# Two adjacency layers on one core: the order of the first batch's opening, and GpSimd for three kinds of small work

## The chip, the cores and the metric

The kernel runs on one core of a Trainium2 chip. A core has TensorE (PE: matrix products, written to the accumulation memory PSUM), VectorE (DVE), ScalarE (ACT), GpSimd (POOL) and SyncE (SP, which here only issues DMAs). Each engine runs its own instructions strictly in order; between engines, order is kept by semaphores. The metric is the device time of one launch in microseconds (us), as the median of several runs.

## The reference

A batch of 16 graphs of 1024 nodes with 128 features passes two layers, both in float32; a layernorm over the features follows the residual addition of each. `adj` holds zeros and ones.

```python
# layer 0, per batch
h = x @ Ww.T + Wb
e = (h @ A) @ h.T;  e = e + e.T
scores = where(adj > 0, e, 0)
attention = softmax(scores, axis=1) * adj        # along the first node index
hp = relu(attention @ h)
ic, fc, oc = (sigmoid(hp @ w_u + x @ w_x) for each gate)
x = layernorm(x + oc * tanh(ic * hp + fc * x))

# layer 1, per batch, 4 heads
h = x @ conv_w + conv_b
Ah = tanh(adj * (h @ attn_w @ h.T))
x = layernorm(x + relu(relu(mean over heads of relu(Ah @ h)) + x))
```

## The kernel before

All work goes in tiles of 128 rows, so a batch has eight row tiles j = 0 to 7 of 128 x 1024 scores. The host passes x also as its transpose `xT`, and adj as `adjT`.

**The weights' chain.** Scores need only the symmetric matrix A + A^T. The kernel makes a_sym = A + A^T, s_ww = a_sym times Ww, and q_w = Ww^T s_ww, so that the scores are products of a query projection `qT` = q_w applied to xT (with a bias column `c_col`) and xT itself; the bias part left over is a column that h carries along. For that the rows of h have G = 132 columns: 128 for h, three for the gates' `x @ w_x`, one for the bias part of the score. The matrix that makes them is `wwT_g`: Ww^T, then `gate_x` (three columns, made by a product of `rows_x` with an identity and a copy), then `c_col`. What is added to each row is `wb_row`: the bias Wb, zeros, and in the last column a number that is made out of `sb_col` = a_sym Wb by one more product (`finish_weights`, L163). Each of these small products is one TensorE instruction pair into a tile of PSUM (the helper `small`, four rotating buffers of 512 columns) and a copy out by VectorE or ScalarE; the chain is lines 142 to 166. Two of them, for `c_col` (L154) and for `sb_col` (L156), write columns of one tile, `p_c`. `gates_x` (L159) is called later, after the first query projection.

**Layer 0 of batch 0** is at the front of the kernel with nothing beside it but the first pieces of batch 1. `layer0` (L283) returns a dictionary of pieces, each a function that issues a few instructions, and the order in which the strings name them is the order in which the instructions stand in every engine's queue. The pieces that matter here, with their lines:

- `Q0`, `Q1` (L306): the two halves of the query projection on TensorE, copied out with the bias: for batch 0 by ScalarE (Q0) and VectorE (Q1).
- `H0` to `H2` (L323) and `h0` to `h2` (L333): products of xT with `wwT_g` for three, three and two row tiles, and VectorE's addition of `wb_row` (L335). The last addition also copies the 24 gate columns out of h (L341).
- `E j` (L391): the edge tile adj > 0. For batch 0 it is made by VectorE in bfloat16, for the others by GpSimd.
- `S j` (L343): the scores of row tile j from the diagonal to the right; ScalarE drains them from PSUM into the big tile `R`, and adds h's last column as bias (L353), so the first drain waits for `h0`. For batch 0, S0 is one piece and S1 is split into S1.0 and S1.1.
- `T j` (L359, L380): the scores left of the diagonal are transposes of earlier ones; for batch 0 by TensorE through PSUM with a copy back by ScalarE (L368, L369, L385, L386).
- `A j` (L401): VectorE masks the row tile and takes its maximum in one instruction (L405), negates the maximum (L410), and ScalarE takes the exponential in place and its sum z (L412). The mask overwrites what `T j` reads, so it waits for that.
- `B j` (L414): VectorE takes 1/z (L420); h over that sum, called `hz`, is made by VectorE for j = 0, 1, 6, 7 of batch 0 (L422) and otherwise by ScalarE (L424); VectorE multiplies the exponentials by adj (L427); and TensorE accumulates row tile j - 1 (`back`, L431, L435), with hz as the weights.
- `R`, `P`, `G`: the last accumulation and relu (L440), the rows of h' (L446), the gates (L499). Inner, outer and norm pieces (I, O, V, N) follow, then batch 0's x for layer 1.

The order of the opening is lines 725 to 767, written by hand, a string per stretch. The loads stand first: xT in two halves, the eight adjacency tiles of batch 0, x, batch 1's xT, the late weights, and batch 1's adjacency tiles, all on SP's queue. ScalarE's queue issues A, Wb as a column and the three `rows_x` (L73 to L80); GpSimd's issues Wb into `wb_row` (L91).

**From there on** the 16 batches go through layer 1 in 32 steps each (`layer1_step`, L613: scores on TensorE, times adj on VectorE, tanh on ScalarE, accumulation on TensorE). Between the steps, two tables by step number (`BETWEEN`, `AHEAD`, L771 and L776) put in the layer 0 pieces of the next two batches. The additions `h0 h1 h2` of a later batch stand at step 14 of `AHEAD`, next to `Y` (a GpSimd product, L467) at step 14 and `F` (GpSimd again, L493) at step 16.

Of the kernel before, what the change touches and what calls it, by code (L numbers as in the profile page):

```python
# [24 lines left out]
def two_layer_adjacency_kernel(  # L25
# [19 lines left out]
    nc = tc.nc  # L45
    B, N, D = x.shape
    H = conv_w.shape[0]
    assert D == P and N % 512 == 0
    NB = N // P
# [11 lines left out]
    def small(name):  # L61
        return ps_sc.tile([P, 512], F32, tag="sc", name=name)
# [4 lines left out]
    ident = consts.tile([P, P], F32, name="ident")  # L67
# [8 lines left out]
    wb_col = consts.tile([P, 1], F32, name="wb_col")  # L76
    nc.scalar.dma_start(wb_col, Wb.rearrange("(d o) -> d o", o=1))
    rows_x = sb.tile([3, P], F32, tag="s1", name="rows_x", bufs=4)
# [14 lines left out]
    gate_u, gate_x = ident_g[:, D : D + 3], wwT_g[:, D : D + 3]  # L93
# [33 lines left out]
    a_sym = sb.tile([P, P], F32, tag="hz", name="a_sym", bufs=4)  # L127
# [3 lines left out]
    sb_col = consts.tile([P, 1], F32, name="sb_col")  # L131
# [10 lines left out]
    pa, pw, ps, pc = small("p_a"), small("p_ww"), small("p_s"), small("p_c")  # L142
# [8 lines left out]
    pq, px = small("p_q"), small("p_x")  # L151
# [1 line left out]
    nc.vector.tensor_copy(q_w, pq[:, :P])  # L153
    nc.tensor.matmul(pc[:, 0:1], s_ww, wb_col, start=True, stop=True)  # L154
    nc.vector.tensor_copy(c_col, pc[:, 0:1])
    nc.tensor.matmul(pc[:, 1:2], a_sym, wb_col, start=True, stop=True)  # L156
    nc.vector.tensor_copy(sb_col, pc[:, 1:2])

    def gates_x():  # L159
        nc.tensor.matmul(px[:, :3], rows_x, ident[:3, :3], start=True, stop=True)  # L160
        nc.vector.tensor_copy(gate_x, px[:, :3])

    def finish_weights():  # L163
        pt = small("p_bsb")
        nc.tensor.matmul(pt[:, :1], b_wide, sb_col, start=True, stop=True)
        nc.vector.tensor_copy(wb_row[:, G - 1 : G], pt[:, :1])

    def join_weights():

        nc.vector.tensor_sub(cw, cw_in, cw_last)  # L170
        pt = small("p_cwT")
        for hd in range(H):
            nc.tensor.transpose(pt[:, ts(hd, P)], cw[:, hd, :], ident)
        nc.scalar.copy(cwT.rearrange("p h f -> p (h f)"), pt)
        yield
        pt = small("p_caT")
        for hd in range(H):
            nc.tensor.matmul(pt[:, ts(hd, P)], aw[:, hd, :], cwT[:, hd, :], start=True, stop=True)
        nc.scalar.copy(caT.rearrange("p h f -> p (h f)"), pt)
        yield  # L180
        pt = small("p_m")
        for hd in range(H):
            nc.tensor.matmul(pt[:, ts(hd, P)], caT[:, hd, :], cwT[:, hd, :], start=True, stop=True)
        nc.scalar.copy(ms.rearrange("p h f -> p (h f)"), pt)
# [98 lines left out]
    def layer0(b):  # L283
# [5 lines left out]
        t = {}  # L289
# [43 lines left out]
        def add_h(g):  # L333
            h, ks = t["h"], GROUPS[g]
            nc.vector.tensor_add(  # L335
                h[:, ks[0] : ks[-1] + 1, :], t["ph", g],
                wb_row.unsqueeze(1).to_broadcast([P, len(ks), G]),
            )
            if g == len(GROUPS) - 1:
                t["gate"] = sb.tile([P, NB, 3], F32, tag="gate", name=f"gate_{b}")  # L340
                nc.vector.tensor_copy(t["gate"], h[:, :, D : D + 3])  # L341

        def score(j, halves=None):  # L343
            if j == 0:
# [69 lines left out]
        def weigh(j):  # L414

            s = t["R"][:, :, j, :]
            adj = adj_t[b, j].rearrange("p (k d) -> p k d", d=P)
            rz = sb.tile([P, 1], F32, tag="rz", name=f"rz_{b}_{j}", bufs=4)
            t["hz", j] = sb.tile([P, D], F32, tag="hz", name=f"hz_{b}_{j}", bufs=4)
            nc.vector.reciprocal(rz, t["z", j])  # L420
            if b == 0 and j in (0, 1, NB - 2, NB - 1):
                nc.vector.tensor_scalar_mul(t["hz", j], t["h"][:, j, :D], rz)  # L422
            else:
                nc.scalar.mul(t["hz", j], t["h"][:, j, :D], rz)  # L424

            for ks in (ts(0, BH), ts(1, BH)) if (b, j) == (0, NB - 1) else [slice(NB)]:
                nc.vector.tensor_mul(s[:, ks], s[:, ks], adj[:, ks])  # L427
            if j:
                back(j - 1)

        def back(j):  # L431
            if j == 0:
                t["acc"] = ps_acc.tile([P, N], F32, tag="acc0", name=f"acc0_{b}")
            for q in range(NH):
                nc.tensor.matmul(  # L435
                    t["acc"][:, ts(q, 512)], t["hz", j], t["R"][:, ts(q, BH), j, :],
                    start=(j == 0), stop=(j == NB - 1),
                )
# [117 lines left out]
        for g in range(len(GROUPS)):  # L556
            pieces[f"H{g}"] = partial(multiply_h, g)
            pieces[f"h{g}"] = partial(add_h, g)
# [7 lines left out]
        for j in range(NB):  # L566
            for name, piece in (
                ("L", load_adj), ("E", find_edges), ("S", score), ("A", mask), ("B", weigh)
            ):
                pieces[f"{name}{j}"] = partial(piece, j)  # L570
            if j + 1 < NB:
                pieces[f"T{j}"] = partial(turn_score, j)
# [4 lines left out]
    def run(pieces, names):  # L577
        for name in names.split():
            if name in pieces:
                pieces.pop(name)()  # L580
# [144 lines left out]
    first, second, join = layer0(0), layer0(1), join_weights()  # L725
# [2 lines left out]
    load_late_weights()  # L728
    run(second, "L0 L1 L2 L3 L4 L5 L6 L7")
    run(first, "Q0")  # L730
    gates_x()
    finish_weights()
    run(first, "E0 H0 h0 E1 E2 S0 T0.0 S1.0 T0.1 S1.1 A0 E3 T1 S2 A1 Q1 E4 H1 h1 B0 T2 S3 A2 E5 B1")
    run(first, "H2 h2 T3 S4 A3 E6 B2")
    run(first, "T4 S5 A4 E7 B3 T5 S6 A5 B4 T6 S7 A6")
    run(second, "Q0")
    run(first, "B5 A7")
    run(second, "H0")
# [136 lines left out]
```

## Time and profile before

| what | value |
|---|---|
| median of 4 runs | 2414.4 us |
| the four runs | 2412.87, 2412.93, 2415.86, 2415.90 us |
| time of the profiled execution | 2412.87 us |
| its span, first to last instruction | 2410.9 us |
| granted TensorE clock, mean | 1.000 |
| TensorE busy | 2398.8 us |
| VectorE busy | 1555.0 us |
| ScalarE busy | 1063.2 us |
| GpSimd busy | 603.3 us |
| GpSimd busy between 5.2 and 47.6 us | 0 |

The profile is one execution as the hardware profiler took it. Busy times are sums of instruction lengths on an engine; in a row of instructions in order of time, the first number is the start in us from the span's start, the second the length; brackets give the idle time of the engine before it, and behind the arrow what ended it. The chain of waits is found by going back from the last instruction: at each step to what released it, or to the instruction before it on its engine. "issue" in it is time in which the engine waited for nothing that the profile shows. Matmul ends are modelled.

### The profile page before, as it was taken

What the parts mean: (1) busy time and instruction counts of PE and PEld (TensorE: products, weight loads), DVE (VectorE), ACT (ScalarE), POOL (GpSimd) and SP (SyncE); (2) the same over time, 40 slices, a digit from 0 to 9 for tenths busy, and PEclk for the clock granted to TensorE, in tenths of its full rate; (3) what the DMA queues carried; (4) which work ended last, traced back from release to release, by engine and by line L of the source; (5) the groups of instructions that cost most, each with busy time, mean ns of one, the idle gap of its engine ahead of it and who ended that gap; (6) DMA issues with size and microseconds to landing.
All of it is one profiled execution on the core that took longest, in us unless ns stands there. A gap on an engine that the chain in (4) does not pass through costs nothing.

```text
span 2410.9 us, 20160 instructions
## 1 busy us (share of the span) xinstructions
PE 2398.8 (100%) x5981; PEld 1095.2 (45%) x5981; DVE 1555.0 (64%) x3280; ACT 1063.2 (44%) x1500; POOL 603.3 (25%) x373
## 2 busy tenths in 40 slices
PE   8999999999999999999999999999999999999999
PEld 5444444444444444444444444444444444444444
DVE  7666666666667666676666665666666576666555
ACT  6544344443444444445344454434444344443333
POOL 1314131241312413123131231312214132141000
PEclk9999999999999999999999999999999999999999
DMA  5334151441514325143242432425234251341010
GB/s 185 79 75 127 36 139 36 95 115 48 127 44 99 102 51 124 49 109 87 60 115 57 113 76 70 105 61 122 62 71 113 53 126 58 79 115 34 18 27 9
DMA packets 474349, 197.04 MB, mean 82 GB/s; under 512 B 414964, under 2 KB 440303, under 8 KB 474240
## 3 DMA queue, kind: packets, MB, share of 16 engines
q1 hardware_dynamic: 455626, 129.03, 22.9%
q0 software_dynamic: 18320, 66.66, 9.4%
q8 instruction: 48, 0.79, 0.1%
q14 instruction: 61, 0.50, 0.1%
q10 hardware_dynamic: 294, 0.07, 0.0%
HBM read 136.19 MB, written 59.51 MB: 81 GB/s over the span
## 4 chain that ended last, share of the span: by engine, by line
PE 98%; DVE 1%; DMA 0%; issue 0%; ACT 0%; POOL 0%; POOLq 0%; DVEq 0%; ACTq 0%
PE sc L630 36%; PE acc L636 36%; PE acc L435 9%; PE sc L350 5%; PE pR L601 5%; PE pT_u L234 5%; PE pR_h L331 1%; PE pT_q L234 1%; DMA adj<-in_adjT_dram 0%; DVE R L405 0%; DVE R L427 0%; DVE st L210 0%; DVE edge L398 0%; DMA a_in<-in_L_gnn_A_dram 0%; DVE u L523 0%
## 5 line engine op out<-in xcount | busy, mean ns | idle before, releaser
L631 DVE TENSOR_TENSOR s<-sc,adj 128x512 f32<-128x512 f32 x1008 | 685.6, 688 | 710.7 <-PE sc L630 689.8
L632 ACT ACTIVATE s<-s 128x1024 f32<-128x1024 f32 x504 | 533.1, 1058 | 1057.4 <-DVE s L631 898.0
L630 PE MATMUL sc<-uT,x1T 128*128 128x512 f32 x2048 | 962.4, 592 | 0.0
L636 PE MATMUL acc<-s,h 128*128 128x512 f32 x2016 | 947.3, 592 | 0.0
L636 PEld LDWEIGHTS acc<-s,h 128*128 128x128 f32 x2016 | 380.5, 190 | 484.7 <-issue 477.5
L630 PEld LDWEIGHTS sc<-uT,x1T 128*128 128x128 f32 x2048 | 386.9, 190 | 469.3 <-issue 403.5
L398 POOL TENSOR_SCALAR edge<-adj 128x1024 uint8<-128x1024 f32 x120 | 332.8, 2774 | 316.1 <-DVE top_None L405 314.0
L214 POOL TENSOR_TENSOR rs<-rs,mhalf 128x8 f32<-128x8 f32 (+3 forms) x35 | 54.0, 1543 | 884.5 <-DVE rs L213 884.5
L435 PE MATMUL acc<-R,hz 128*128 128x512 f32 x512 | 240.8, 593 | 2.3 <-DVE R L427 1.4
L412 ACT ACTIVATE R<-R,nmax 128x1024 f32<-128x1024 f32 x128 | 147.0, 1148 | 84.8 <-DVE nmax L410 75.5
L405 DVE CUSTOM_DVE_ANT_0 R<-R,edge 128x1024 f32<-128x1024 f32 (+1 forms) x128 | 154.8, 1209 | 0.5 <-PE turn L368 0.5
L427 DVE TENSOR_TENSOR R<-R,adj 128x1024 f32<-128x1024 f32 x129 | 154.5, 1198 | 0.0
L435 PEld LDWEIGHTS acc<-R,hz 128*128 128x128 f32 x512 | 96.6, 190 | 124.7 <-issue 115.0
L350 PE MATMUL sc<-xT,qT 128*128 128x512 f32 (+3 forms) x384 | 145.2, 487 | 0.5 <-ACT R L369 0.3
L353 ACT ACTIVATE R<-sc,h 128x512 f32<-128x512 f32 (+1 forms) x192 | 110.7, 580 | 52.0 <-PE sc L350 44.3
L467 POOL TENSOR_TENSOR x1T<-hp,wu_b 128x1024 f32<-128x1024 f32 x45 | 106.3, 2362 | 103.5 <-DVE hws L473 63.7
L234 PE MATMUL pT_u<-x1T,ms 128*128 128x512 f32 x256 | 120.5, 592 | 0.0
L601 PE MATMUL pR<-cw,x1T 128*128 128x512 f32 x256 | 117.6, 598 | 0.0
L350 PEld LDWEIGHTS sc<-xT,qT 128*128 128x128 f32 x384 | 69.6, 190 | 69.6 <-issue 59.8
L300 POOL DMA_DIRECT2D adj<-in_adjT_dram x112 | 65.7, 587 | 92.6 <-DVE s L631 92.6
L654 DVE SCALAR_TENSOR_TENSOR sum<-acc,sum 128x512 f32<-128x512 f32 x95 | 61.3, 687 | 42.1 <-PE acc L636 42.1
L604 ACT COPY h<-pR 128x512 f32<-128x512 f32 x128 | 72.4, 592 | 27.9 <-PE pR L601 26.2
(144 smaller groups left out, 1127.7 us busy)
## 6 DMA issues: line engine op xcount, KB each, us to landing
adj<-in_adjT_dram POOLq DMA_DIRECT2D x112, 512.0 KB, 4.0
adj<-in_adjT_dram SPq DMA_DIRECT2D x16, 512.0 KB, 8.2
x<-in_x_dram SPq DMA_DIRECT2D x16, 512.0 KB, 5.3
xT<-in_xT_dram SPq DMA_DIRECT2D x15, 512.0 KB, 4.8
dram_hp<-turn_hp SPq DMA_DIRECT2D x15, 512.0 KB, 2.6
hp<-dram_hp SPq DMA_DIRECT2D x60, 128.0 KB, 3.3
dram_x<-turn_x SPq DMA_DIRECT2D x15, 512.0 KB, 3.1
x1T<-dram_x SPq DMA_DIRECT2D x60, 128.0 KB, 5.7
```

Of the source, the lines that this page charges most:

```text
L234: nc.tensor.matmul(ps, w, src[:, ts(q, 512)], start=True, stop=True)
L350: nc.tensor.matmul(ps[:, : at - lo], t["qT"][:, ts(j, P)], t["xT"][:, lo:at], start=True, stop=True)
L398: engine.tensor_scalar(m, adj_t[b, j], 0.0, None, ALU.is_gt)
L405: nc.vector.tensor_tensor_reduce(s[:, ks], s[:, ks], t["edge", j][:, ks], 1.0, nmax, ALU.mult, ALU.max, top)
L412: nc.scalar.activation(s, s, AF.Exp, bias=nmax, accum_out=t["z", j])
L427: nc.vector.tensor_mul(s[:, ks], s[:, ks], adj[:, ks])
L435: nc.tensor.matmul(t["acc"][:, ts(q, 512)], t["hz", j], t["R"][:, ts(q, BH), j, :], start=(j == 0), stop=(j == NB - 1),)
L601: nc.tensor.matmul(ps, x1T_t[b][:, ts(k, P)], cw.rearrange("p h d -> p (h d)"), start=True, stop=True)
L630: nc.tensor.matmul(ps, x1T[:, ts(m, P)], uT[:, ts(q, 512)], start=True, stop=True)
L631: nc.vector.tensor_mul(s[:, ts(q, 512)], ps, adj[:, ts(q, 512)])
L632: nc.scalar.activation(s, s, AF.Tanh)
L636: nc.tensor.matmul(acc[:, ts(q, 512)], h1[:, ts(hd, D)], s[:, ts(q, 512)], start=(m == 0), stop=(m == NB - 1),)
```

## The change

- The gate product and its copy (`rows_x` into `gate_x`) move from behind the first query projection into the weights' chain, straight after `c_col`. The product for `sb_col` takes the place behind the projection, now as `weigh_bias`, and writes a column of the gates' tile `p_x` instead of `p_c`.
- `H0` is issued ahead of `finish_weights`, and `h0` ahead of the first edge tile `E0`.
- The edge tiles are spread anew: E1 and E2 stand behind A0 instead of ahead of S0, and every later one moves one place back. `Q1` moves from behind A1 to ahead of T1.
- hz of batch 0 is made by GpSimd for all eight row tiles. The gate columns of every batch are copied by GpSimd.

```diff
     nc.vector.tensor_copy(c_col, pc[:, 0:1])
-    nc.tensor.matmul(pc[:, 1:2], a_sym, wb_col, start=True, stop=True)
-    nc.vector.tensor_copy(sb_col, pc[:, 1:2])
-
-    def gates_x():
-        nc.tensor.matmul(px[:, :3], rows_x, ident[:3, :3], start=True, stop=True)
-        nc.vector.tensor_copy(gate_x, px[:, :3])
+    nc.tensor.matmul(px[:, :3], rows_x, ident[:3, :3], start=True, stop=True)
+    nc.vector.tensor_copy(gate_x, px[:, :3])
+
+    def weigh_bias():
+        nc.tensor.matmul(px[:, 3:4], a_sym, wb_col, start=True, stop=True)
+        nc.vector.tensor_copy(sb_col, px[:, 3:4])
...
                 t["gate"] = sb.tile([P, NB, 3], F32, tag="gate", name=f"gate_{b}")
-                nc.vector.tensor_copy(t["gate"], h[:, :, D : D + 3])
+                nc.gpsimd.tensor_copy(t["gate"], h[:, :, D : D + 3])
...
             nc.vector.reciprocal(rz, t["z", j])
-            if b == 0 and j in (0, 1, NB - 2, NB - 1):
-                nc.vector.tensor_scalar_mul(t["hz", j], t["h"][:, j, :D], rz)
+            if b == 0:
+                nc.gpsimd.tensor_scalar_mul(t["hz", j], t["h"][:, j, :D], rz)
             else:
                 nc.scalar.mul(t["hz", j], t["h"][:, j, :D], rz)
...
     run(first, "Q0")
-    gates_x()
+    weigh_bias()
+    run(first, "H0")
     finish_weights()
-    run(first, "E0 H0 h0 E1 E2 S0 T0.0 S1.0 T0.1 S1.1 A0 E3 T1 S2 A1 Q1 E4 H1 h1 B0 T2 S3 A2 E5 B1")
-    run(first, "H2 h2 T3 S4 A3 E6 B2")
-    run(first, "T4 S5 A4 E7 B3 T5 S6 A5 B4 T6 S7 A6")
+    run(first, "h0 E0 S0 T0.0 S1.0 T0.1 S1.1 A0 E1 E2 Q1 T1 S2 A1 E3 H1 h1 B0 T2 S3 A2 E4 B1")
+    run(first, "H2 h2 T3 S4 A3 E5 B2")
+    run(first, "T4 S5 A4 E6 B3 T5 S6 A5 E7 B4 T6 S7 A6")
     run(second, "Q0")
     run(first, "B5 A7")
```

## The prediction

> **What bounds the kernel now.** I read the page first, its busy table, its slices and its shares of the chain. The span is TensorE's from end to end but for the first slice.
>
> ```profile
> span 2410.9 us, 20160 instructions
> ...
> PE 2398.8 (100%) x5981; PEld 1095.2 (45%) x5981; DVE 1555.0 (64%) x3280; ACT 1063.2 (44%) x1500; POOL 603.3 (25%) x373
> ...
> PE 98%; DVE 1%; DMA 0%; issue 0%; ACT 0%; POOL 0%; POOLq 0%; DVEq 0%; ACTq 0%
> ```
>
> The chain cut to its first 75 us shows where the other 2% lie: pieces with start, length and engine.
>
> ```profile
> 2.94 6.71 DMA adj<-in_adjT_dram
> ...
> 9.67 0.07 DVE edge L398
> ...
> 10.28 0.57 DVE h L335
> ...
> 10.94 0.70 ACT R L353
> ...
> 37.22 0.30 ACT hz L424
> ...
> 37.56 5.55 PE acc L435 x12
> ```
>
> Up to 9.65 the chain waits for the first adjacency tile; then the edge tile and h's first addition stand in line, ScalarE's first score (L353) waits for that addition, VectorE carries 18 to 35 us, and TensorE's last accumulations close batch 0. From 57 on TensorE has no gap, so whatever the first 57 us gain or lose goes to the end unchanged. The changed lines act there, apart from a copy of 24 columns per batch.
>
> Third view: VectorE's instructions in order of time; brackets hold the idle time before and what ended it.
>
> ```profile
> 9.67 0.69 DVE L398 TENSOR_SCALAR edge<-adj 128x1024 bf16<-128x1024 f32 x1 [1.13 <-DMA adj<-in_adjT_dram]
> 10.28 0.56 DVE L335 TENSOR_TENSOR h<-pR_h,wb_row 128x396 f32<-128x396 f32 x1
> ...
> 15.75 1.23 DVE L405 CUSTOM_DVE_ANT_0 R<-R,edge 128x1024 f32<-128x1024 f32 x1 [0.51 <-PE turn L368]
> ...
> 17.79 0.75 DVE L312 TENSOR_SCALAR qT<-pT_q_second,wwT_g 128x512 f32<-128x512 f32 x1 [0.62 <-PE pT_q_second L311]
> ...
> 19.73 0.29 DVE L422 TENSOR_SCALAR hz<-h,rz 128x128 f32<-128x128 f32 x1
> 19.93 1.22 DVE L427 TENSOR_TENSOR R<-R,adj 128x1024 f32<-128x1024 f32 x1
> 21.07 1.22 DVE L405 CUSTOM_DVE_ANT_0 R<-R,edge 128x1024 f32<-128x1024 f32 x1
> ```
>
> The reader sees gaps until 17.79, none that matter from there to 40.9, and that one hz on VectorE sits between a reciprocal and a product. I call mask j "A j", product j "B j" (reciprocal, hz, product), edge tile j "E j".
>
> **Step 1, the weights' chain.** Now the product for c_col, the one for sb_col (both in tile p_c, so the second waits 0.33 for c_col's copy, until 6.37) and the first query projection at 6.62 follow each other. Afterwards the gate product in its own tile px takes the second place. It needs rows_x: the last packets of ScalarE's DMA queue, which brings it, fall at 5.25 to 5.3; wb_col on the same queue landed at 4.77, some 0.5 after its last packets. So rows_x lands between 5.3 and 7.65 (where it was used), and I take 5.8, by wb_col's row. TensorE is free for it at 5.97: no wait. q_w's copy ends at 6.25, so the projection starts at about 6.35 (-0.27). Behind it by the old durations: sb_col's product at 7.36, h's first products 7.67 (0.66 for six), the bias product 8.33, the first scores 8.72 instead of 9.06. The copies between are 0.16 each and beside this (sb_col's ends at 7.94, before 8.33). The bias column is in wb_row at about 8.9; the other columns landed at 1.61 + 6.6 = 8.2. h's addition then runs 8.93 to 9.49, wholly in the wait for the adjacency tile, instead of ending at 10.84. The first score lasts 1.02 on TensorE, so ScalarE drains it from 9.77 instead of 10.94: -1.17.
>
> **Step 2, to mask 1.** The alternation of TensorE and ScalarE (turn, score, drain) keeps its durations; its second turn needs the second drain, and the shift is -1.14 at the last score of row 1 (drain at 13.07, before 14.21). A 0 no longer stands behind E 1 and E 2: 10.5 to 12.3. E 1, E 2 follow to 13.5 (tile 2 had landed by 12.2). The second query projection, 0.86 of TensorE, is now ahead of turn 1: at 12.87 to 13.73, while turn 1's larger half waits for the drain ending at 13.76 anyway; turn 1 loses 0.14. Its copy-out with bias on VectorE is done at 14.6. A 1 starts at 14.75 instead of 15.75: -1.0.
>
> **Step 3, mask 1 to mask 2.** From 15.75 to 21.07 before: A 1 1.42, a gap 0.62 for the projection, its addition 0.67, an edge tile 0.60, h's second addition 0.48, B 0 with hz 1.53. Afterwards: A 1 1.33, E 3 0.60, the addition 0.48, B 0 without hz 1.20 (as 27.04 to 28.24, where hz was ScalarE's). 14.75 + 3.61 = 18.36 instead of 21.07: -2.71. The addition's products on TensorE end at 16.5, before it needs them.
>
> **Step 4, mask 2 to the last product.** VectorE is without gaps, so instructions count. From 21.07 to B 7's start at 39.27 were 18.20; two hz go (0.33 each, 1.53 less 1.20) and the gate copy (0.12, from 24.99 to 25.11); one more edge tile comes in (four behind A 2 where there were three: +0.60). 18.02, so B 7 at 36.38: -2.89. B 7 then waits: exponential 7 is complete 1.48 after the negation of its maximum began (37.68 to 39.16), B 6 covers only 1.27 of that. Of these 0.25 nothing reaches the end: TensorE's accumulation 6 starts at 36.4 and lasts 1.72, until 38.1, and B 7's first half is out at 36.38 + 0.25 + 0.76 = 37.4.
>
> **Step 5, hz by GpSimd.** No row has this multiplication there. Bounds: a 128x128 copy takes 0.29 on POOL; the 128x4 multiplication takes 0.25, and the edge tile's slope, (2.77 - 0.25) x 124/1020 = 0.31, on top gives 0.56. I take 0.35, an eighth of the edge tile, also a tensor-scalar form. GpSimd is idle from 5.1 to 47.7, so nothing is queued behind. TensorE waits for hz together with the product, which takes 1.2 behind the same reciprocal, in halves for the last: all of 0.56 is covered, and up to about 1.0 would be. Four hz also leave ScalarE (0.39 each); the fifth had stood there behind an exponential and held TensorE from 37.14 to 37.56. That is part of the same 2.89, not on top.
>
> Whether GpSimd's reading delays VectorE is the open price. For no: POOL's edge tile beside the same products.
>
> ```profile
> 70.13 2.77 POOL L398 TENSOR_SCALAR edge<-adj 128x1024 uint8<-128x1024 f32 x1 [6.42 <-DVE top_None L405]
> ```
>
> ```profile
> 72.03 1.20 DVE L427 TENSOR_TENSOR R<-R,adj 128x1024 f32<-128x1024 f32 x1
> ```
>
> They overlap from 72.03 to 72.90, the product keeps its 1.20, and all 120 edge tiles lie between 2.76 and 2.80. For yes: of L492's two multiplications on VectorE one takes 286 ns, the other, beside a GpSimd product, 641. So 0 to 0.355 per hz; I take 0, since the first rows have the operation that will stand beside hz. [...]
>
> **Step 6, the rest.** relu starts at 43.15 - 2.89, and the chain to 57 moves with it: convolution weights (29.8 + 4.7 = 34.5) and the second batch's xT (21.6) are in long before. Batch 1's gate copy leaves VectorE at 50.94, but the next instruction (L534, 51.08) needs a tanh ending at 51.05: nothing. In the other batches VectorE is not the bound (PE row: no gap), and on GpSimd the copy (0.2 to 0.3 estimated from the 128x4 row) waits for h (137.9) between a product ending at 136.2 and one starting at 147.1: nothing is held. No DMA is moved, added or passed; the SP queue issues as before.
>
> **Sum.** -2.89, say -2.9 us. The profiled execution took 2412.87 (span 2410.9 and 1.97 around), so its like would take 2410.0. It is one of a lower pair (2412.87, 2412.93); the upper pair is 2415.86 and 2415.90, the median 1.5 above the profile. For the median: 2414.4 - 2.9 = 2411.5, 0.12% less; 0.2% (4.8 us) is about what can be told from no change.
>
> **Rivals.** (a) *Waits take the place of the instructions.* With VectorE shorter, its reciprocals may wait for ScalarE's exponentials, or turns stand behind accumulations on TensorE. For it: 0.25 at B 7, and ScalarE was 4.89 of 5.00 busy in 15 to 20. Against: 2.63 in 20 to 25. Then only step 2's 1.0 remains: 2413.4. (b) *rows_x is late*, at 7.65: the projection then starts at 7.9, 1.55 later than I have it, and the forecast keeps 2.9 - 1.55 = 1.35: 2413.1. Against: those packets. (c) *Slower: GpSimd's hz blocks VectorE.* The place is the mask behind each product. At 0.355 (L492) eight cost 2.84 and all is level, 2414.4; at the upper 0.56 they cost 4.5 and the time is 2414.4 - 2.9 + 4.5 = 2416.0. It decides from 2.9/8 = 0.36 each. (d) *The change does not do what it says*: h's addition starts no earlier, because the column from the bias product is late. It would have to come 1.3 later than 8.9 to give back step 1; that is contained in (b)'s price.
>
> **How the numbers follow.** Forecast 0.62, (a) 0.19, (b) with (d) 0.07, (c) 0.12. Given the forecast, steps 2 to 4 can be off by 1 each way, and the median can fall on either pair (1.5 each way): 2409.5 to 2413.5 is its own range. For 8 in 10 the low end is 2414.4 - 2.9 - 1.5 - 1.0 = 2409.0; the high end is (a) in the upper pair, 2415.9 - 1.0 = 2414.9, say 2415.0, which takes in the level case of (c). Faster by over 0.2% means under 2409.6: a quarter of the forecast's chance, when both the sum and the pair fall well, 0.16. Slower by over 0.2%, above 2419.2, needs (c) at twice its price or a cost that I do not see: 0.07. Within: 0.77.
>
> **What would show it.** In the changed profile: h's addition ends before the first edge tile starts; the first L353 starts near 9.8; mask 1 near 14.75 and mask 2 near 18.4; no VectorE gap from there to B 7 but one of about 0.25; hz on POOL at 0.3 to 0.56 and products still at 1.2; relu near 40.3; convolution rows and layer 1 some 2.9 earlier. It is wrong if the projection L317 waits for rows_x, if the masks lengthen or start late behind hz, if reciprocals wait for ScalarE before B 7, or if TensorE's gap-free stretch starts at 57 as before because something in 40 to 57 is bound elsewhere.

## The result and the profile after

The changed kernel takes 2416.53 us (median of 40 runs) and the kernel before 2413.0 us (60 runs beside them): 1.0014 times the time, with a 95% interval of 1.0009 to 1.0018. The forecast was 2411.5, with 2409.0 to 2415.0 as the range. The kernel became slower by 3.5 us instead of faster by 2.9, and the time lies above the range. The profiled execution took 2416.11 us with a span of 2414.3, against 2412.87 and 2410.9 before, so it shows 3.2 of those 3.5 us. One thing is needed for the medians below: the runs of most kernels fall into two to four groups that lie one to three microseconds apart, in different shares from kernel to kernel (one of the changed kernel's 40 lies far out, at 2525.06), so differences under about 1.5 us between medians of 11 runs are not taken as shown.

The page of the changed kernel, with its span, its busy table and its shares of the chain:

```profile
span 2414.3 us, 20175 instructions
...
PE 2400.7 (99%) x5981; PEld 1096.8 (45%) x5981; DVE 1551.2 (64%) x3260; ACT 1062.5 (44%) x1496; POOL 622.7 (26%) x397
...
PE 98%; DVE 1%; POOL 0%; ACT 0%; DMA 0%; issue 0%; ACTq 0%; POOLq 0%; DVEq 0%
```

TensorE is busy 1.9 us longer than before and still idle for more of the span (2414.3 - 2400.7 = 13.6, before 12.1). VectorE lost 3.8 us of work and GpSimd took on 19.4, of which hz is 16. That alone says that the eight hz took 2 us each on average, not the forecast 0.35.

The chain of waits of the changed kernel, cut to its first 75 us: start, length, engine.

```profile
2.47 4.59 DMA rows_x<-in_L_gnn_wo_x_dram
7.20 0.35 PE p_x L156 x2
...
19.51 1.22 DVE R L405
...
21.72 2.56 PE acc L435 x4
...
31.72 3.04 POOL hz L422
34.81 1.98 PE acc L435 x4
36.79 0.12 PE turn L368
36.94 1.23 DVE R L405
...
38.62 2.49 POOL hz L422
41.15 5.42 PE acc L435 x12
```

Before, the chain began with the adjacency tile and then stood on VectorE from 18 to 35. Now it begins with `rows_x`, and from 21.7 it alternates between GpSimd's hz, TensorE's accumulations and the masks. The last twelve accumulations begin at 41.15, before at 37.56: 3.6 us later.

GpSimd's instructions on line 422 in order of time (start, length; in brackets the idle time before and what ended it):

```profile
18.66 4.53 POOL L422 TENSOR_SCALAR hz<-h,rz 128x128 f32<-128x128 f32 x2 [13.83 <-PE turn L368]
...
28.43 1.43 POOL L422 TENSOR_SCALAR hz<-h,rz 128x128 f32<-128x128 f32 x1 [2.53 <-DVE rz L420]
31.72 4.55 POOL L422 TENSOR_SCALAR hz<-h,rz 128x128 f32<-128x128 f32 x2 [1.87 <-DVE rz L420]
38.62 5.47 POOL L422 TENSOR_SCALAR hz<-h,rz 128x128 f32<-128x128 f32 x3 [2.34 <-DVE rz L420]
```

One hz took 1.41 at least, 1.43 in the median and 3.03 at most. Set beside VectorE's rows, each ends only behind VectorE's work: hz of tile 2 runs 28.43 to 29.86, beside the product from 28.17 to 29.38, and ends 0.5 behind it; hz of tile 3 runs 31.72 to 34.76, through the product at 31.47, the mask at 32.59 and the edge tile at 33.93 to 34.61, and ends 0.15 behind that. Three of the eight are long: tiles 0 and 3 (3.0) and tile 5 (2.5). They are the three that TensorE waits for.

Its accumulations on the same rows of time:

```profile
21.72 2.56 PE L435 MATMUL acc<-R,hz 128*128 128x512 f32 x4 [2.08 <-POOL hz L422]
...
34.81 1.98 PE L435 MATMUL acc<-R,hz 128*128 128x512 f32 x4 [2.27 <-POOL hz L422]
...
41.15 5.42 PE L435 MATMUL acc<-R,hz 128*128 128x512 f32 x12 [0.77 <-POOL hz L422]
```

Together 5.1 us. Before, the waits at the accumulations were for products and ScalarE and came to 0.54 + 0.84 + 0.52 + 0.43 = 2.3:

```profile
21.20 1.98 PE L435 MATMUL acc<-R,hz 128*128 128x512 f32 x4 [0.54 <-DVE R L427]
...
28.47 1.95 PE L435 MATMUL acc<-R,hz 128*128 128x512 f32 x4 [0.84 <-DVE R L427]
...
31.59 1.95 PE L435 MATMUL acc<-R,hz 128*128 128x512 f32 x4 [0.52 <-ACT R L369]
...
37.56 5.55 PE L435 MATMUL acc<-R,hz 128*128 128x512 f32 x12 [0.43 <-ACT hz L424]
```

And VectorE waits for TensorE, because the third addition's products, the turns and the scores are queued behind these accumulations:

```profile
9.85 0.57 DVE L335 TENSOR_TENSOR h<-pR_h,wb_row 128x396 f32<-128x396 f32 x1
10.34 0.68 DVE L398 TENSOR_SCALAR edge<-adj 128x1024 bf16<-128x1024 f32 x1
12.06 0.69 DVE L405 CUSTOM_DVE_ANT_0 R<-R,edge 128x512 f32<-128x512 f32 x1 [1.04 <-PE turn L385]
...
15.86 1.21 DVE L405 CUSTOM_DVE_ANT_0 R<-R,edge 128x1024 f32<-128x1024 f32 x1
...
19.51 1.22 DVE L405 CUSTOM_DVE_ANT_0 R<-R,edge 128x1024 f32<-128x1024 f32 x1
...
25.20 0.43 DVE L335 TENSOR_TENSOR h<-pR_h,wb_row 128x264 f32<-128x264 f32 x1 [2.48 <-PE pR_h L331]
26.16 1.22 DVE L405 CUSTOM_DVE_ANT_0 R<-R,edge 128x1024 f32<-128x1024 f32 x1 [0.53 <-PE turn L368]
...
36.94 1.23 DVE L405 CUSTOM_DVE_ANT_0 R<-R,edge 128x1024 f32<-128x1024 f32 x1 [1.13 <-PE turn L368]
```

Masks 3 and 6 before:

```profile
25.11 1.22 DVE L405 CUSTOM_DVE_ANT_0 R<-R,edge 128x1024 f32<-128x1024 f32 x1
...
33.89 1.22 DVE L405 CUSTOM_DVE_ANT_0 R<-R,edge 128x1024 f32<-128x1024 f32 x1
```

The reader can follow the whole loss in the masks. Mask 2 starts at 19.51, still 1.56 ahead of before (21.07). Mask 3 starts at 26.16, 1.05 behind (25.11). Mask 6 starts at 36.94, 3.05 behind (33.89). The last reciprocal stands at 42.34 (39.27), the relu stage at 46.60 (43.15), and 3.4 us is also what the span grew by. So the opening gained, and the two gaps behind hz of tile 0 and of tile 3 cost 2.6 and 2.0.

Another loss is hidden in the first of these gaps. The accumulation at 21.72 took 2.56 instead of 1.98 for four matmuls, and from its start to the end of the turn behind it TensorE needed 4.30 us (21.72 to 26.02), where the same work took 2.87 before (21.20 to 24.07): about 1.4 of the 2.6. The table by stretches of time (length of the stretch; busy time and count of TensorE, its weight loads, VectorE, ScalarE, GpSimd; then the granted clock of TensorE, the DMA share and GB/s) shows why:

```profile
18.00:23.00 5.00, 2.92 (x11) 1.49 (x12) 4.69 (x9) 3.71 (x8) 4.25 (x2) 1.00 0.52 154
23.00:26.00 3.00, 3.00 (x11) 2.25 (x10) 0.43 (x1) 0.00 (x0) 0.40 (x2) 0.50 0.09 25
```

From 23 on, 1.3 us after an idle time of 2.08 had ended, the clock was granted at 0.50 for about three microseconds. Before, it stands at 1.00 in both stretches, and behind the second gap of the changed kernel, 2.27 long, it stayed at 1.00 too.

### The profile page after: what moved, and what is told of

The parts are those of the page before. It is cut to its first block, busy times and chain, and to the rows that moved or that the text cites. A ratio compares the mean times of both kernels' runs of the same rounds, so it can differ in the third digit from the quotient of the medians.

```text
span 2414.3 us, 20175 instructions
## 1 busy us (share of the span) xinstructions
PE 2400.7 (99%) x5981; PEld 1096.8 (45%) x5981; DVE 1551.2 (64%) x3260; ACT 1062.5 (44%) x1496; POOL 622.7 (26%) x397
## 4 chain that ended last, share of the span: by engine, by line
PE 98%; DVE 1%; POOL 0%; ACT 0%; DMA 0%; issue 0%; ACTq 0%; POOLq 0%; DVEq 0%
PE sc L630 36%; PE acc L636 36%; PE acc L435 9%; PE sc L350 5%; PE pR L601 5%; PE pT_u L234 5%; PE pR_h L331 1%; PE pT_q L234 1%; POOL hz L422 0%; DVE R L405 0%; DMA rows_x<-in_L_gnn_wo_x_dram 0%; DVE st L210 0%; PE pt L454 0%; DVE edge L398 0%; PE pt L593 0%
```

## The experiments

The theory from these rows: hz on GpSimd is held back while VectorE runs its products and masks, ends after the product instead of beside it, and TensorE, whose queue holds the next tile's turn behind the accumulation, passes the delay on to the masks. Rivals: the new order of the pieces or the weights' chain (`rows_x` late) costs the time; or GpSimd simply needs 1.4 us for this form of instruction, beside VectorE or not; or it delays VectorE, as rival (c) of the prediction has it.

All times are medians. Each ratio is to the kernel before, run beside it on the same chip; it is not exactly the ratio of the two medians (for chain_as_before those give 1.0020, for order_alone 0.9999).

| kernel | us | lowest | before, same chip | ratio, 95% |
|---|---|---|---|---|
| changed, again | 2416.38 | 2415.14 | 2412.99 | 1.0013, 1.0004 to 1.0022 |
| hz_as_before | 2411.75 | 2410.57 | 2412.94 | 0.9995, 0.9986 to 1.0004 |
| hz_alone | 2417.47 | 2417.06 | 2412.94 | 1.0020, 1.0011 to 1.0029 |
| chain_as_before | 2417.79 | 2414.40 | 2412.94 | 1.0015, 1.0006 to 1.0024 |
| order_alone | 2412.60 | 2411.89 | 2412.87 | 1.0002, 0.9993 to 1.0010 |
| gate_alone | 2412.50 | 2412.12 | 2412.87 | 0.9999, 0.9990 to 1.0008 |
| busy_gap | 2411.56 | 2410.89 | 2412.87 | 0.9996, 0.9987 to 1.0005 |
| rz_ahead | 2411.16 | 2410.57 | 2412.87 | 0.9994, 0.9985 to 1.0003 |
| filled | 2411.26 | 2410.65 | 2412.99 | 0.9992, 0.9983 to 1.0000 |
| gates_behind | 2411.26 | 2410.95 | 2412.99 | 0.9993, 0.9984 to 1.0002 |

**hz_as_before: the changed kernel with hz where it was.**

```diff
-            if b == 0:
-                nc.gpsimd.tensor_scalar_mul(t["hz", j], t["h"][:, j, :D], rz)
+            if b == 0 and j in (0, 1, NB - 2, NB - 1):
+                nc.vector.tensor_scalar_mul(t["hz", j], t["h"][:, j, :D], rz)
```

> The changed kernel with one part undone: hz of batch 0 is made by VectorE (tiles 0, 1, 6, 7) and ScalarE (2 to 5) again; everything else stays changed. Theory 1 (hz on GpSimd is what costs: in the changed profile each takes 1.41 to 3.03 us instead of the forecast 0.35, and TensorE waits for it 2.08, 2.27 and 0.77 us): those waits go, mask 2 starts near 19.8 (0.33 for hz back on VectorE), the last product near 38.5 instead of 39.3 before, and the time is 0.7 us below the kernel before, about 4 us below the changed one. Theory 2 (the late rows_x in front of the query projection, and TensorE's clock of 0.50 from 23 to 26 us, cost it whatever engine makes hz): the time stays 2 us or more above the kernel before.

Measured: 2411.75, so undoing this one part takes 4.8 us off the changed kernel (4.7 with each held against the kernel before beside it) and leaves it level with the kernel before or 1.2 ahead. TensorE's waits at the accumulations are for products and ScalarE again, the first 0.34 instead of 2.08; the last is as long as in the changed kernel (0.81 and 0.77), but for ScalarE's hz:

```profile
23.04 1.98 PE L435 MATMUL acc<-R,hz 128*128 128x512 f32 x4 [0.34 <-DVE R L427]
...
39.76 5.55 PE L435 MATMUL acc<-R,hz 128*128 128x512 f32 x12 [0.81 <-ACT hz L424]
```

The order of the pieces and the weights' chain are in this kernel, and it is not slower: they are not where the 3.5 us went. (The rows are of an execution of 2414.92 with a slow opening, so their start times are not to be held against those above; the last section comes back to it.)

**hz_alone: the kernel before with hz by GpSimd and nothing else.** The edit is the one above in the other direction, on the kernel before.

> The kernel before with one part of the change alone: hz of batch 0 by GpSimd for all eight tiles. Theory 1: hz takes 1.4 to 3 us here too, TensorE's accumulations wait for it, and the turns and masks queued behind them with it: 2 to 4.5 us slower than before, although VectorE is rid of four hz (1.3 us). Theory 2: no slower, down to 1.3 us faster.

Measured: 2417.47, 4.5 us more than before. It has the same waits with the old order of pieces, and the same slow accumulation behind the first:

```profile
22.93 3.51 PE L435 MATMUL acc<-R,hz 128*128 128x512 f32 x4 [2.28 <-POOL hz L422]
...
32.85 1.98 PE L435 MATMUL acc<-R,hz 128*128 128x512 f32 x4 [1.98 <-POOL hz L422]
...
39.41 1.98 PE L435 MATMUL acc<-R,hz 128*128 128x512 f32 x4 [1.01 <-POOL hz L422]
```

Taking it out (-4.8) and putting it in (+4.5) agree: this part is necessary and sufficient for the loss.

**chain_as_before: the changed kernel with the old weights' chain**, the gates' product behind the projection again.

```diff
-    nc.tensor.matmul(px[:, :3], rows_x, ident[:3, :3], start=True, stop=True)
-    nc.vector.tensor_copy(gate_x, px[:, :3])
+    nc.tensor.matmul(pc[:, 1:2], a_sym, wb_col, start=True, stop=True)
+    nc.vector.tensor_copy(sb_col, pc[:, 1:2])
...
-    weigh_bias()
+    gates_x()
```

> The changed kernel with the weights' chain put back (sb_col's product ahead of the query projection, the gates' product behind it); the new order of the pieces, hz and the gate copy on GpSimd stay. Theory 1: rows_x, which landed at 7.06 in the changed profile, no longer holds the projection (7.48 becomes 6.6), and some 0.7 to 0.9 us of it reach the end, so about 2.5 us above the kernel before. Theory 2 (rows_x is most of the loss): 3 us or more off the changed kernel's time, level with before or below. If the wait was hidden: as the changed kernel, 3.4 above before.

Measured: 2417.79, no better than the changed kernel (2416.53), with the waits for hz in place (2.09, 1.95, 1.24). Neither the 2.5 above before of the first theory nor the level time of the second came; the wait for `rows_x` is not what costs the time.

**probe: the disputed cost by itself.** GpSimd multiplies 128x128 by a column (as hz does), by a constant, by a broadcast second input, copies it, or compares a 128x1024 tile as the edge tile is made; beside it VectorE does nothing, three products of two SBUF inputs, three masks, six products with one input from PSUM, or six compares with one SBUF input.

```diff
+    def beside_two(n):
+        for _ in range(n):
+            nc.vector.tensor_mul(big[2], big[1], big[0])
...
+    def beside_psum(n):
+        for _ in range(2 * n):
+            nc.vector.tensor_mul(big[2][:, :512], acc, big[0][:, :512])
...
+    def pool_pointer(rz):
+        o = pooled[:, :P]
+        nc.gpsimd.tensor_scalar_mul(o, hsrc, rz)
+        return o
```

> No part of the layers is computed: a program of small stretches only. In each, VectorE makes a scalar, then runs three long instructions of one kind (none; products of two SBUF tensors; masks with maximum; products of PSUM and SBUF; compares with one SBUF input to bfloat16), while GpSimd runs one instruction that waits for the scalar: a 128x128 multiplication by a pointer scalar, by a constant, by a broadcast tensor, a copy, and the 128x1024 compare. In a second half VectorE has one short instruction ahead of the long ones. Theory A (VectorE instructions with two SBUF inputs keep GpSimd's reads out): 0.3 to 0.56 us alone, over 1.4 us beside products and masks for all the 128x128 forms, and again 0.3 to 0.56 beside products with PSUM. Theory B (the pointer scalar itself is slow): 1.4 us in every stretch for the pointer form alone, and under 0.6 for the others. Theory C (the pointer form alone is kept out): only the pointer form goes over 1.4 us, and only beside products or masks; constant form and 128x1024 compare keep their time, as the edge tiles do in the profile before.

GpSimd's rows of the column form, in the order nothing, products, masks, PSUM products, compares:

```profile
8.20 0.61 POOL L104 TENSOR_SCALAR pooled<-hsrc 128x128 f32<-128x128 f32 x1 [7.77 <-DVE hsrc L135]
9.09 1.50 POOL L104 TENSOR_SCALAR pooled<-hsrc 128x128 f32<-128x128 f32 x1 [0.29 <-DVE hsrc L135]
12.86 1.57 POOL L104 TENSOR_SCALAR pooled<-hsrc 128x128 f32<-128x128 f32 x1 [2.26 <-DVE hsrc L135]
16.70 0.60 POOL L104 TENSOR_SCALAR pooled<-hsrc 128x128 f32<-128x128 f32 x1 [2.27 <-DVE hsrc L135]
21.04 1.42 POOL L104 TENSOR_SCALAR pooled<-hsrc 128x128 f32<-128x128 f32 x1 [3.74 <-DVE hsrc L135]
```

The operation takes 0.61 alone. Beside instructions of VectorE that read two SBUF tiles, and beside the compares, it takes 0.8 to 1.0 more; beside products that read one of their inputs from PSUM it takes nothing more. The other forms have the same step: the constant 0.53 alone and 1.43 beside the products, the broadcast input 0.40 and 1.31, the copy 0.29 and 1.22, the edge compare 2.78 and 3.60. So it is not a slow form of instruction: GpSimd is held up beside VectorE's instruction. In the column form it loses 0.89 beside products and 0.96 beside masks, and what was left of VectorE's 1.2 us when it began (0.18 and 0.13 behind it) was 1.0 and 1.1. Where GpSimd starts first (VectorE has a short PSUM instruction ahead), it keeps its 0.61, 0.53, 0.40 and 0.29 beside products and masks; beside the compares the first two forms were still held (1.64 and 0.98). VectorE pays little for these short ones, its three products taking 3.74 to 3.85 in all; beside the long compare it pays 0.8:

```profile
150.62 4.49 DVE L87 TENSOR_TENSOR big<-big,big 128x1024 f32<-128x1024 f32 x3
...
155.59 2.04 DVE L92 CUSTOM_DVE_ANT_0 big<-big,bit 128x1024 f32<-128x1024 f32 x1
...
157.68 1.22 DVE L92 CUSTOM_DVE_ANT_0 big<-big,bit 128x1024 f32<-128x1024 f32 x1
```

The mask that started just behind GpSimd's compare of 2.77 us (at 155.52) was held for 0.82 (2.04 less 1.22), not for the whole 2.77.

**rz_ahead: hz stays on GpSimd but starts earlier.** In the changed kernel the reciprocal and hz are one call with the product; here, for tiles 0 to 4, they are issued straight behind the next tile's mask, ahead of the edge tile.

```diff
-        def weigh(j):
-
-            s = t["R"][:, :, j, :]
-            adj = adj_t[b, j].rearrange("p (k d) -> p k d", d=P)
+        def share(j):
...
+        def weigh(j):
+
+            s = t["R"][:, :, j, :]
+            adj = adj_t[b, j].rearrange("p (k d) -> p k d", d=P)
+            if ("hz", j) not in t:
+                share(j)
...
-    run(first, "H2 h2 T3 S4 A3 E5 B2")
...
+    run(first, "H2 h2 T3 S4 A3 r2 E5 B2")
...
```

> The changed kernel, hz still on GpSimd, but for tiles 0 to 4 the reciprocal and hz are issued straight behind the mask of the next tile, ahead of an edge tile or h's addition, instead of straight ahead of the product. Theory 1 (GpSimd's read is shut out while VectorE runs a product, a mask or an edge tile, and gets in at the seams): hz still shows 1 to 1.5 us, but ends before its product does; TensorE's waits for hz of 2.08 and 2.27 us go, and the time falls by 3 to 5 us below the changed kernel, to 2411 to 2413. Theory 2 (GpSimd's own length, or its shutting out VectorE, is what costs): the time stays within 1.5 us of the changed kernel.

Measured: 2411.16, 1.7 us below the kernel before beside it, where the changed kernel is 3.5 above: 5.2 us less, and the lowest median of all, though the interval of its ratio still takes in 1. Of the five hz that were moved, three are longer than in the changed kernel (1.94 and 1.95 instead of 1.43) and two shorter (tile 0: 0.89 instead of 3.01; tile 3: 1.95 instead of 3.03), and TensorE waits for them for 0.58 at most (1.11 for tile 5, which was left as it was). GpSimd, then TensorE:

```profile
25.75 1.94 POOL L419 TENSOR_SCALAR hz<-h,rz 128x128 f32<-128x128 f32 x1 [0.38 <-DVE rz L417]
28.97 1.95 POOL L419 TENSOR_SCALAR hz<-h,rz 128x128 f32<-128x128 f32 x1 [1.27 <-DVE rz L417]
```

```profile
24.40 1.88 PE L438 MATMUL acc<-R,hz 128*128 128x512 f32 x4
...
27.75 1.98 PE L438 MATMUL acc<-R,hz 128*128 128x512 f32 x4 [0.50 <-POOL hz L419]
...
37.98 5.42 PE L438 MATMUL acc<-R,hz 128*128 128x512 f32 x12 [1.11 <-POOL hz L419]
```

So what counts is when hz ends, not how long it takes: with one edge tile (0.6) more between reciprocal and product, an hz of 1.95 is covered nearly to its end.

**order_alone: only the new order of the pieces**; hz, the gate copy and the weights' chain are as before.

```diff
+    run(first, "H0")
...
-    run(first, "E0 H0 h0 E1 E2 S0 T0.0 S1.0 T0.1 S1.1 A0 E3 T1 S2 A1 Q1 E4 H1 h1 B0 T2 S3 A2 E5 B1")
...
+    run(first, "h0 E0 S0 T0.0 S1.0 T0.1 S1.1 A0 E1 E2 Q1 T1 S2 A1 E3 H1 h1 B0 T2 S3 A2 E4 B1")
...
```

> The new order of the pieces alone: h's first products and addition ahead, edge tiles behind, the second query projection ahead of turn 1; the weights' chain, hz and the gate copy as before. Theory 1 (the forecast's steps 2 to 4 hold, less the 0.99 of three hz that stay on VectorE in the counted stretch, and less what the old chain costs): 1.5 to 2 us below the kernel before, compared at the lowest groups of runs of both. Theory 2 (turn and drain set the opening whatever VectorE's order): level within 0.5.

Measured: 2412.60 against 2412.87 beside it, so the 1.5 to 2 us of the first theory did not come; the lowest runs are 0.7 apart (2411.89 and 2412.61). The order alone is worth nothing that can be told from zero; its interval allows up to 1.7.

**gate_alone: the kernel before with the gate copy by GpSimd.**

```diff
-                nc.vector.tensor_copy(t["gate"], h[:, :, D : D + 3])
+                nc.gpsimd.tensor_copy(t["gate"], h[:, :, D : D + 3])
```

> The kernel before with the gate copy of all 16 batches on GpSimd, nothing else. Theory 1 and 2 agree: level with the kernel before within 0.3 us, one copy of 0.12 us leaves VectorE's opening and TensorE bounds the rest. If GpSimd's copies delayed later GpSimd work: slower by some 0.1 us for each of 16 batches or more.

Measured: 0.9999 of before. The sixteen gate copies cost and bring nothing that can be told from zero, though a copy that falls beside a mask takes 1.13 to 1.14 on GpSimd (rz_ahead, hz_as_before) instead of 0.20 (the changed kernel).

**busy_gap: hz_as_before with idle matmuls in the wait for `rows_x`.**

```diff
+    keep_at_work(1)
     nc.tensor.matmul(px[:, :3], rows_x, ident[:3, :3], start=True, stop=True)
```

> The changed kernel with hz back on VectorE and ScalarE, and one more product of zeros on TensorE between c_col's product and the gates' product, where TensorE waits 0.45 to 0.77 us for rows_x. Theory 1 (the spread of runs, 2410.6 to 2415.3, comes from TensorE running its first products at half speed until a stretch without gaps, as the 2.08 instead of 1.12 us of the first projection shows): with the gap filled more runs fall in the lowest group, median 2410.8 or less. Theory 2 (the spread has another source): the same groups in the same shares, median 2411.7.

Measured: 2411.56, where hz_as_before had 2411.75: nothing. Nine of its eleven runs lie within 2410.89 to 2411.85, and two at 2415.0, as in hz_as_before with its two near 2415. The idle time in the opening is not what sets these runs apart. This kernel's profiled execution, 2411.34, is the one to hold against the profile of before (2412.87): mask 1 starts at 15.41, mask 2 at 19.40 and the last reciprocal at 37.97, 1.30 ahead of before, and the time is 1.5 less.

**filled: rz_ahead with tile 5 early too, and the gap filled** (the edit against rz_ahead).

```diff
+    keep_at_work(1)
...
-    run(first, "T4 S5 A4 r3 E6 B3 T5 S6 A5 r4 E7 B4 T6 S7 A6")
+    run(first, "T4 S5 A4 r3 E6 B3 T5 S6 A5 r4 E7 B4 r5 T6 S7 A6")
```

> As rz_ahead, with the reciprocal and hz of tile 5 ahead too (behind product 4, ahead of mask 6), and one product of zeros in TensorE's wait for rows_x. Theory (both costs of the change are those found: hz shut out, and a gap in TensorE's work before the projection that lets its rate fall to half for some 4 us): the wait of 1.11 us for hz 5 shrinks to under 0.5, no half-speed stretch follows the gap, and the median is 2409.5 to 2410.5. Rival (the rate falls whatever fills the gap): groups as in rz_ahead, median 2410.7 to 2411.2.

Measured: 2411.26, not the 2409.5 to 2410.5 of the theory. The wait for hz of tile 5 is gone, but tile 6 took it over with 0.93. Shortening one wait uncovered the next, and the time is that of rz_ahead.

**gates_behind: the gates' product behind the projection**, with the product for `sb_col` in the tile `p_x` ahead of it, so that neither waits for `rows_x` nor for `c_col`'s copy; hz as in filled.

```diff
-    nc.tensor.matmul(px[:, :3], rows_x, ident[:3, :3], start=True, stop=True)
-    nc.vector.tensor_copy(gate_x, px[:, :3])
+    nc.tensor.matmul(px[:, 3:4], a_sym, wb_col, start=True, stop=True)
+    nc.vector.tensor_copy(sb_col, px[:, 3:4])
...
-    weigh_bias()
+    gates_x()
```

> As rz_ahead with tile 5's reciprocal ahead too, and the gates' product behind the query projection again, but with sb_col's product in the gates' tile in its place ahead: TensorE waits neither for rows_x nor for c_col's copy there. Theory (rows_x in front of the projection cost 0.66 to 0.77 us of wait, and half speed behind it in some runs): the projection starts near 6.4 and the median is 2409.5 to 2410.3. Rival (that wait was hidden): level with the kernel that fills the gap.

Measured: 2411.26, the same median as filled, as the rival said. Against the changed kernel the projection starts at 6.67 instead of 7.48, but h's addition and the first mask move by only 0.24. TensorE, then VectorE:

```profile
6.67 1.10 PE L317 MATMUL pT_q_first<-xT,q_w 128*128 128x512 f32 x2
...
8.32 0.94 PE L331 MATMUL pR_h<-wwT_g,xT 128*128 128x132 f32 x6 [0.25 <-DVE wwT_g L161]
```

```profile
9.61 0.57 DVE L335 TENSOR_TENSOR h<-pR_h,wb_row 128x396 f32<-128x396 f32 x1
...
11.82 0.69 DVE L405 CUSTOM_DVE_ANT_0 R<-R,edge 128x512 f32<-128x512 f32 x1 [1.04 <-PE turn L385]
```

The gates' product now delays h's products from its new place (0.25 for its copy), and the first mask still waits 1.04 for the first turn.

**changed_again: the changed kernel itself, beside the last two.**

> The changed kernel itself beside the others of this call, so that they are compared on one chip: 2415.5 to 2418.5, median near 2416.5.

Measured: 2416.38, 1.0013 of before, with waits for hz of 2.09, 1.95 and 1.57. The result repeats, and the versions with an earlier reciprocal are 5.1 us below it on the same chip. In this execution two stretches of lower clock (granted 0.83 from 18 to 23, 0.71 from 23 to 26, then 0.72 from 30 to 36) fall on the accumulations behind the first two of these waits, which take 3.62 and 3.44 instead of 1.98.

## Why the prediction was wrong

The forecast for the start of the relu stage was 43.15 - 2.89 = 40.26; it came at 46.60. The 6.34 us between them divide by the prediction's own steps:

| step | forecast | measured | error, us |
|---|---|---|---|
| 1 and 2, to mask 1 | 14.75 | 15.86 | +1.11 |
| 3, mask 1 to mask 2 | 3.61 | 3.65 | +0.04 |
| 4 and 5, mask 2 to the last reciprocal | 18.02 | 22.83 | +4.81 |
| last reciprocal to relu | 3.88 | 4.26 | +0.38 |

**Step 5 failed, and it alone turned the sign.** (Of the 4.81, 0.23 is the wait at the last product, which the prediction kept out of this sum.) It took hz at 0.35, set 0.56 as the upper bound, took 0 for contention and said that up to about 1.0 would be covered. Alone the operation takes 0.61 (probe), already above the bound, because the bound was scaled down from a compare with a constant, and the form that takes its factor from a column costs 0.08 more; this error would have been covered. In the kernel it took 1.41 to 3.03. The statement on the cover was right in kind: TensorE waits for hz together with a product of 1.2, and what goes beyond is paid. That 0 was taken for the contention is the error that counts. The row it leaned on, GpSimd's edge tile from 70.13 beside a product at 72.03, was true and did not bear on the case. In the probe, a compare that starts first held up a mask just behind it by 0.82 of its 2.77 us; the product at 72.03 came 1.9 us in. And in the changed kernel hz does not start first: its reciprocal ends as the product begins, so VectorE has the start, by 0.24 to 0.27 in each of the eight. The prediction looked at a like pair of instructions in the wrong order of starting. Two of its own signs of being wrong came: the projection waited for `rows_x` (0.77), and masks started late behind hz.

The probe shows which side pays for this form: where VectorE's products started first, GpSimd's 0.61 became 1.50 and the three products took 3.79; where GpSimd started first, it kept its 0.61 and they took 3.83. The prediction priced the wrong side of it, GpSimd holding up VectorE at 0 to 0.355 per hz, and took 0 because of one row.

**Rival (c) had nearly the number, 2416.0, and the wrong mechanism.** It expected masks delayed behind each product. They are not: masks keep 1.21 to 1.23, with one of 1.36 at 29.32. It is GpSimd that is held, and TensorE's order of work that passes it on, so that its number came near is luck.

**Where the stall went** was missed with it: the prediction priced the contention on VectorE's masks alone, and rival (a), which names turns that stand behind accumulations, only as a lost gain (2413.4). TensorE's accumulation stands ahead of the third addition's products and of the next turn, so the hz of tile 0, for which TensorE waited 2.08, left the third addition waiting for 2.48 and mask 3 for 0.53, and that of tile 3 (2.27) left mask 6 waiting for 1.13. The clock granted at 0.50 after the first of these gaps, about 1.4 of the 4.81, was not in any step. In changed_again, with two such stretches, TensorE took 21.42 from the accumulation of tile 0 to that of tile 5 (21.11 to 42.53), in the changed kernel's first profile 19.43 (21.72 to 41.15).

**Step 1: the mechanism was right, a size was off.** `rows_x` was taken to land at 5.8, and landed at 7.06; the projection began at 7.48, not 6.35, h's addition at 9.85, not 8.93. This is rival (b), with 7.06 in place of its 7.65. The size varies with the execution: in changed_again the projection began at 6.86 and the first turn at 10.74, 0.62 earlier than here (7.48 and 11.36). h's addition was to lie wholly in the wait for the first adjacency tile and end at 9.49; it ended at 10.42, and the first edge tile started at 10.34, 0.67 later than before.

**Step 2 missed a wait.** Mask 0 was put at 10.5, behind the first edge tile. It began at 12.06, 1.04 of it a wait for the turn, because mask 0 overwrites what the turn reads. It was the edge tiles E1 and E2 ahead of it that covered this before.

**Steps 3, 4 and 6 held.** Mask 1 to mask 2 took 3.65 (3.61 forecast); the wait before the last product came as 0.23 (0.25 forecast); the gate copy costs nothing (gate_alone). Without the waits for hz, the profiled execution of busy_gap puts the last reciprocal 1.30 ahead of before and takes 1.5 less. Of the 1.59 that are missing to the forecast at that place, 0.66 were lost up to mask 1 (15.41 against 14.75), 0.38 from there to mask 2 (3.99 against 3.61) and 0.55 behind it (18.57 against 18.02). This kernel keeps on VectorE one hz in the second stretch and two in the third, at the prediction's 0.33 each, so these two are its hz and the first is steps 1 and 2.

**The base was off too.** The four runs put the kernel before at 2414.4, between two groups; 60 runs put it at 2413.0. With every step right the time would have come to 2410.1, not to 2411.5.

What stays open: how much of these 1.2 to 1.7 us in the medians belongs to the order, the chain and the freed VectorE. No run separates them by more than its interval. Also open is what makes TensorE's opening matmuls long in one execution and short in another, which is worth some 3.5 us (last section); filling the gap did not remove it.

## What to carry to other kernels

Before an instruction is given to GpSimd beside VectorE work, look at which one starts first and what VectorE reads from SBUF at that time: here a short operation that started just behind a long VectorE instruction with two SBUF inputs ended behind it, whatever it cost alone (in the probe 0.29 to 0.61 alone, 1.22 to 1.50 behind products). Look then at when the consumer comes: issue the input earlier, so that the consumer comes later than the end of VectorE's work (rz_ahead: 5.2 us less, with three of the five moved hz even longer), or don't move it. And a row of "both run at full speed" counts only if the two started in the same order, and as close together, as they will after the change.

## What was not expected of the hardware

- GpSimd's 128x1024 compare keeps VectorE out for about 0.8 of its 2.8 us only: the mask behind it took 2.04 instead of 1.22, and three products 4.49 instead of 3.73; six compares by VectorE took 5.75 instead of 4.37. A compare by VectorE that reads one SBUF tile shuts GpSimd out too: the two multiplications by a scalar as long as a product does (0.61 to 1.42, 0.53 to 1.39), the other two short forms about half as long (0.40 to 0.78, 0.29 to 0.69).
- Where VectorE's instructions follow each other closely, GpSimd may not get in between them: hz of tile 3 waited through a product, a mask and an edge tile (3.03), as did hz of tile 0 (3.01), while hz of tile 2, in the same place of its row, got in behind one product (1.43), and the mask behind that took 1.36 instead of 1.22. What decides between the two is not shown.
- Idle gaps of about 2 us on TensorE were followed by a granted clock of 0.50 in some cases and not in others. The four profiles with hz late (the changed kernel, changed_again, hz_alone, chain_as_before) have eight gaps of 1.95 to 2.28: behind five the clock fell and the accumulation took 2.56 to 3.62, behind three it took its 1.98. Summed over the windows of the tables, each of these five stretches lasted 3.4 us (what is missing to a clock of 1.00, doubled). Nor did the length of the gap tell slow from fast in the opening: h's first six products took 1.67 in rz_ahead (a gap of 0.66 ahead of them) and 1.62 in order_alone (gaps of 0.33 and 0.25), but 0.92 in the changed kernel (0.77).
- The opening can run slow without a sign in the clock row. The first projection's two matmuls took 2.08 in the profiled execution of hz_as_before and 1.12 in that of the changed kernel, with a granted clock of 1.00 there in both tables:

```profile
7.69 2.08 PE L317 MATMUL pT_q_first<-xT,q_w 128*128 128x512 f32 x2
```

  Why one execution opens like that and another does not, no run shows. What such an opening costs can be read from two pairs of profiles: in filled (first projection 2.08) the accumulation of tile 6 begins 3.44 later than in gates_behind (1.10), which has the same median, at 41.53 against 38.09, and the times of the two executions are 3.46 apart, 2414.74 and 2411.28; in hz_as_before (2.08) and busy_gap (1.13) the last twelve accumulations begin 3.51 apart and the times are 3.58 apart.
- A small DMA took 4.59 us from issue to landing at the start of the kernel (`rows_x`, issued at 2.47, landed at 7.06), though the profile of before had the last packets of its queue at 5.3. In the changed kernel's own profile they fall at 6.3 to 6.5. The last packets of one execution were a poor sign of when the tile can be read in another.
